# Last stage of a gated two-layer network: normed rows turned by VectorE in squares of 32, norm by ScalarE, one core

## The chip, the cores and the metric

The kernel runs on one core of a Trainium2 chip. Five instruction streams work beside each other: TensorE (PE in the profile; PEld is its weight load, which overlaps the matmuls), VectorE (DVE), ScalarE (ACT), GpSimd (POOL) and SyncE (SP), which starts transfers. Each takes its instructions in the order in which they stand in its queue and waits for the others by semaphores. The metric is the device time of one execution, in microseconds; the time before is the median of three runs.

## The reference, cut to what matters

Four layers work on `x` of 16 batches x 256 rows x 256 columns, each of them on the layernorm of the rows: cross attention, a routed feed-forward layer, masked cross attention, and a gated linear attention. The last of them is the stage that the change touches:

```
x = x + tanh(g_ffn[1]) * L1_ffn(layernorm(x))

L1_ffn(x):                     # x: [16, 256, 256], 8 heads of 64, 4 experts, chunks of 64
  q1, k1, v = x @ Wq, x @ Wk, x @ Wv
  q2 = x @ Wqa @ Wqb;  k2 = softmax(x @ Wka @ Wkb)
  gk1, gk2 = log_sigmoid(x @ Wg1a @ Wg1b + bg1) / 16, log_sigmoid(x @ Wg2a @ Wg2b + bg2) / 16
  e = softmax(x @ We);  the highest of 4 gives mask and factor
  o = gla(q1, k1, v, gk1) + sum over experts of gla(q2 * factor, k2 * factor, v, gk2 * mask)
  o = o * rsqrt(mean(o * o) + eps) * norm_w
  g = x @ Wga @ Wgb
  return (o * silu(g)) @ Wo
```

Every product with `x` needs the normed rows turned, columns across the partitions: that is the tile `xnT` below.

## The kernel before

Rows of a batch lie as a tile of 128 partitions x 2 x 256 (`xs[b]`, fp32). The stages run one after the other over all batches; stage 0 (the first attention, with the routing of the second layer beside it) takes the first 970 us or so, stages 1 and 2 end near 1240 us, the last stage's loop fills the rest. There `stage3_fast` (line 1615) is a generator whose first steps run inside the stage before.

**The loop.** Its index `p` runs from 0 to 63 (line 2015): four places per batch `b = p // 4`, place `p % 4` for a pair of heads. In each place the body issues, in this order: `start` steps, `shares` (PE: `den`), the second half of `masked` for p - 1 (DVE), `copies`, `shares_end`, in odd places `gated` (DVE: `u`), `keys_queries(p + 1)` (PE: `kq`), `middle`, `rest`, `decays(p + 1)` (PE `gq`, `gz`; ACT `ee`), `late`, `products(p, 0)` (PE `sc`), `masked(p, 0)` (DVE `at`), `behind_mask`, `factors(p + 1)` (DVE `f`), `by_rows`, `second` and `factors_second` for p + 1 (PE, ACT `e`, POOL `k`, DVE `q`), `logs`, `products(p, 1)` (PE `sc`) and `values(p - 1)` (PE `o`). In the second and third place `values` stands ahead of `second`.

**Order.** From the last stage on, every compute instruction is kept in program order on its engine (`Pinned`, line 42; `matmul` and `transpose`, lines 1632 to 1636). So the tables of steps below set the order of each queue. The profile shows all instructions of `Pinned` under line 50, the matmuls of the last stage under line 1633 and its PE transposes under line 1636.

**The tables** (lines 1968 to 1977): a place, the step, the distance `d` to the batch it works on, and arguments. `run` (line 1979) calls a step only where batch `b + d` exists.

```
start = {0: [(turn, 1)], 2: [(turn_hot, 1)]}
rest = {0: [(bias, 2)], 1: [(route, 1)], 2: [(steepest, 1, 0), (stats, 2)], 3: [(steepest, 1, 1)]}
behind_mask = {0: [(route_logits, 1)], 3: [(norm, 2)]}
logs = {0: [(route_sums, 1), (outgates_end, 0, 0)], 1: [(gate_logs, 1, 0)], 2: [(gate_logs, 1, 1)],
        3: [(outgates_end, 0, 1)]}
```

**The steps on the way of a batch's rows.** `bias` (POOL) adds to `xs[b + 2]` in the first place; `stats` in the third takes mean and variance (DVE) and makes `rs` of them (four POOL instructions: scale, and minus mean times scale); `norm` in the fourth writes `xn` with two DVE instructions that subtract the mean and multiply; `turn` in the first place of the next batch, one batch ahead, turns `xn` with four PE transposes of 128 x 128 into a PSUM bank, `tr`, which ACT copies to `xnT`. `lows(b + 1)` in the same place reads it first, then `vals` in the fourth, and `keys_queries` from there on to the third place of the batch itself.

**Buffers.** `xn` has one buffer. `xnT` has two, one for even and one for odd batches (`of`, line 1621; `w1` is opened anew at line 1999). The PSUM banks of `bank` (line 1625) are two in the loop, taken in turn by `tr`, `den`, `low`, `rt`, `zg`, `z`, `ms`, `hT`, `both`, `proj` and `v`. `sc`, the scores of `products`, has one buffer of two banks, so a `products` waits until the `masked` before it has read.

**The same work elsewhere.** `Route.turn` (line 407) with a portion turns rows in stage 0 by DVE: a square of 32 partitions x 32 columns at a place of the grid, for both halves of rows and both halves of columns in one instruction of 32 x 128, sixteen of them for a batch. `normed` (line 219) makes a norm by ACT: two instructions with scale and bias from `rs`.

Of the kernel before, what the change touches and what calls it, by code (L numbers as in the profile page):

```python
# [10 lines left out]
F32 = mybir.dt.float32  # L11
# [6 lines left out]
P = 128  # L18
B, S, D = 16, 256, 256
# [7 lines left out]
def bc(ap, shape, *axes):  # L27

    for a in axes:
        ap = ap.unsqueeze(a)  # L30
    return ap.to_broadcast(list(shape))
# [42 lines left out]
def layers(ctx: ExitStack, tc: tile.TileContext, t, out, check):  # L74
# [11 lines left out]
    xs, cs = [None] * B, [None] * B  # L86
# [17 lines left out]
    w0 = s0.enter_context(tc.tile_pool(name="s0w", bufs=1))  # L104
# [70 lines left out]
    dve, act, pool, pe = (Pinned(tc, x) for x in (nc.vector, nc.scalar, nc.gpsimd, nc.tensor))  # L175
# [43 lines left out]
    def normed(dst, src, mv, rs, p=P, n=2):  # L219
        for i in range(n):  # L220
            act.activation(dst[:, i, :], src[:, i, :], AF.Identity, bias=rs[:p, 1, i:i + 1],
                           scale=rs[:p, 0, i:i + 1])

    def softmax_last(pool, tag, src, shape):

        a = shape[1]
        mx = st.tile([P, a], F32, tag=tag + "mx", name=tag + "mx")
        dve3.tensor_reduce(mx, src, AX.X, ALU.max)
        e = pool.tile(shape, F32, tag=tag, name=tag)
        dve3.tensor_tensor(e, src, bc(mx, shape, 2), ALU.subtract)  # L230
        act3.activation(e, e, AF.Exp)
        den = st.tile([P, a], F32, tag=tag + "den", name=tag + "den")
        dve3.tensor_reduce(den, e, AX.X, ALU.add)
        dve3.reciprocal(den, den)
        pool3.tensor_tensor(e, e, bc(den, shape, 2), ALU.mult)
        return e
# [151 lines left out]
    class Route:  # L388
# [17 lines left out]

        def turn(self, b, bank, portion=None):
            if portion:

                if b not in self.xnT:  # L410
                    self.xnT[b] = ws1.tile([P, 2, S], F32, tag="rxnT", name="rxnT")
                xnT, xn = self.xnT[b], self.xn[b]
                for n in range(*portion):
                    q, r = n // 4 * 32, n % 4 * 32
                    dve.transpose(xnT[r:r + 32].rearrange("p k (i s) -> p i k s", i=2)[:, :, :, q:q + 32],
                                  xn[q:q + 32].rearrange("p i (k d) -> p i k d", k=2)[:, :, :, r:r + 32])
                return
            xnT, xn = ws1.tile([P, 2, S], F32, tag="rxnT", name="rxnT"), self.xn[b]
            self.xnT[b] = xnT
            ps = bank("rtr")  # L420
            for k in range(2):
                for i in range(2):
                    pe.transpose(ps[:, (2 * k + i) * P:(2 * k + i + 1) * P], xn[:, i, k * P:(k + 1) * P], ident)
            act.copy(xnT, ps.rearrange("p (k s) -> p k s", k=2))
# [120 lines left out]
    if fast:  # L545
        route = Route()
# [1068 lines left out]
    def stage3_fast(early_bank):  # L1615

        with ExitStack() as sx:
            w0 = w1 = sx.enter_context(tc.tile_pool(name="f3w0", bufs=1, side="right", reuse_waits="tile"))
            pss = None

            def of(b):

                return w1 if b % 2 else w0

            def bank(name):
                return pss.tile([P, 512], F32, tag="ps", name=name) if pss else early_bank(name)
# [8 lines left out]
            def transpose(*a):  # L1635
                tc.keep_in_program_order(nc.tensor.transpose(*a))
# [11 lines left out]
            xn, xnT, low, lg, hT, em, am = {}, {}, {}, {}, {}, {}, {}  # L1648
# [3 lines left out]
            mvs = {}  # L1652
# [7 lines left out]
            def norm(b):  # L1660
                x = xn[b] = w0.tile([P, 2, D], F32, tag="xn", name="xn")
                mv, rs = mvs.pop(b)
                for i in range(2):
                    dve.tensor_scalar(x[:, i, :], xs[b][:, i, :], mv[:, i, 0:1], rs[:, 0, i:i + 1],
                                      ALU.subtract, ALU.mult)

            def turn(b):
                xnT[b] = of(b).tile([P, 2, S], F32, tag="xnT", name="xnT")
                ps = bank("tr")
                for k in range(2):  # L1670
                    for i in range(2):
                        transpose(ps[:, (2 * k + i) * P:(2 * k + i + 1) * P], xn[b][:, i, k * P:(k + 1) * P], ident)
                act3.copy(xnT[b], ps.rearrange("p (k s) -> p k s", k=2))

            def lows(b):

                low[b] = of(b).tile([P, 2, S], F32, tag="low", name="low")
                ps = bank("low")
                for c in range(2):
                    for k in range(2):  # L1680
                        matmul(ps[:, c * S:(c + 1) * S], la[:, k, c * P:(c + 1) * P], xnT[b][:, k, :],
                                         start=k == 0, stop=k == 1)
                dve3.tensor_copy(low[b][:, 0, :], ps[:, :S])
                dve3.tensor_scalar(low[b][:, 1, :], ps[:, S:], vec[:, V_ONE:V_ONE + 1], None, ALU.add)
                if b > 0:
                    for r in range(0, 64, 32):
                        dve3.tensor_scalar(low2[r:r + 32, :], ps[64 + r:96 + r, S + P:],
                                           vec[64 + r:96 + r, V_ONE:V_ONE + 1], None, ALU.add)
# [149 lines left out]
            def shares(p):  # L1838

                ps = bank("den")  # L1840
                for i in range(2):
                    matmul(ps[:, 2 * i:2 * i + 2], e2[p][:, tokens(i)], halves[:, 0::64],
                                     start=True, stop=True)
                z_[p, "den"] = ps
# [34 lines left out]
            def masked(p, n):  # L1879
                b, m, cols = place(p)  # L1880
                ps = z_.pop((p, n, "sc"))
                a = w2.tile([P, 2, 384], F32, tag=f"at{n}", name=f"at{n}")
                if n == 0:
                    at[p] = a
                    dve3.tensor_tensor(a, ps[:, :, :384], bc(amask, [P, 2, 384], 1), ALU.mult)
                else:
                    r = rd.pop(p)
                    for lo, hi, i in ((0, S, 0), (S, 3 * P, 1)):
                        for j in range(2):
                            dve3.scalar_tensor_tensor(a[:, j, lo:hi], ps[:, j, lo:hi], r[:, 2 * i + j:2 * i + j + 1],  # L1890
                                                           am[b][:, lo:hi], ALU.mult, ALU.mult)
                    if p == last - 1:
                        at[p] = a
                        return
                    pool3.tensor_tensor(at[p], at[p], a, ALU.add)
# [65 lines left out]
            def warm():  # L1961

                ps = bank("warm")
                for _ in range(2):
                    matmul(ps, ones, v[B - 1][:, 0, :], start=True, stop=True)


            start = {0: [(turn, 1)], 2: [(turn_hot, 1)]}
            copies = {2: [(turned_hot, 1)]}
            middle = {0: [(lows, 1)], 1: [(all_gates, 1)], 2: [(pairs, 1)], 3: [(scaled, 0, 0)]}  # L1970

            rest = {0: [(bias, 2)], 1: [(route, 1)], 2: [(steepest, 1, 0), (stats, 2)], 3: [(steepest, 1, 1)]}
            late = {1: [(scaled, -1, 1)], 2: [(project, -1)], 3: [(vals, 1)]}
            behind_mask = {0: [(route_logits, 1)], 3: [(norm, 2)]}
            by_rows = {0: [(outgates, 0, 0)], 1: [(gates_end, 1)], 3: [(outgates, 0, 1)]}
            logs = {0: [(route_sums, 1), (outgates_end, 0, 0)], 1: [(gate_logs, 1, 0)], 2: [(gate_logs, 1, 1)],
                    3: [(outgates_end, 0, 1)]}

            def run(steps, p):
                for f, d, *a in steps.get(p % 4, ()):  # L1980
                    if 0 <= p // 4 + d < B:
                        f(p // 4 + d, *a)
# [30 lines left out]
                    squares((p - 1) // 4, (p - 1) % 4 // 2)  # L2013

            for p in range(last):
                run(start, p)
                shares(p)
                if 0 < p:
                    masked(p - 1, 1)
                run(copies, p)  # L2020
                shares_end(p)
                if 1 < p and p % 2 == 1:
                    gated((p - 2) // 4, (p - 2) % 4 // 2)
                if p + 1 < last:
                    keys_queries(p + 1)
                run(middle, p)
                run(rest, p)
                if p + 1 < last:
                    decays(p + 1)
                run(late, p)  # L2030
                products(p, 0)
                masked(p, 0)
                run(behind_mask, p)
                if p + 1 < last:
                    factors(p + 1)
                run(by_rows, p)

                inside = p % 4 in (1, 2) and p + 1 < last
                if inside:
                    summed(p)  # L2040
                if p + 1 < last:
                    second(p + 1)
                    factors_second(p + 1)
                run(logs, p)
                products(p, 1)
                if 0 < p and not inside:
                    summed(p)

            b, p = B - 1, last - 1
# [126 lines left out]
```

## Time and profile before

| | |
|---|---|
| median of three runs | 1887.42 us (1886.46 to 1890.54) |
| the profiled execution, whole time | 1884.3 us |
| its span | 1882.4 us |
| granted TensorE clock, mean of the span | 0.998 |
| PE transposes `tr` of the last stage | 64, median 273 ns |
| DVE norm `xn` of the last stage | 32, median 406 ns |
| ACT copy of `tr` to `xnT` (two stages) | 32, median 585 ns |
| busy per 40 us of the loop (1520 to 1560) | PE 40.00, DVE 26.11, ACT 18.84, POOL 18.51 us |

A timeline line reads: start (us from the span's start), duration, engine, line, operation, what is written from what, shape, how many merged into the line, and in brackets the idle time of the engine before it with what ended it. A merged line's duration is that of the whole group. A line on a tile gives minimum, median and maximum of one instruction in ns and the first and last start.

### The profile page before, as it was taken

How to read it: one execution, taken by the hardware profiler on the slowest of the kernel's cores; microseconds unless marked ns; L12 is line 12 of the kernel's file. 1: busy time of each engine (PE TensorE's matmuls, PEld its weight loads, DVE VectorE, ACT ScalarE, POOL GpSimd, SP SyncE). 2: the span in 40 equal slices, each digit the busy share in tenths (PEclk: the TensorE clock that was granted, in tenths of full speed). 3: DMA queues.
4: the chain of work that ended last, by engine and by line, in shares of the span. 5: the costliest groups of instructions: out<-in, count | busy, mean ns of one | idle time of the engine just before them, and what ended most of it. 6: DMA issues, size and time to landing. Idle time of an engine off the chain costs nothing.

```text
span 1882.4 us, 35167 instructions
## 1 busy us (share of the span) xinstructions
PE 1857.9 (99%) x13862; PEld 1301.3 (69%) x13862; DVE 1142.9 (61%) x2787; ACT 858.6 (46%) x1790; POOL 1024.0 (54%) x1049
## 2 busy tenths in 40 slices
PE   8999999999999999999999999999999999999997
PEld 5666676666666666666787766567777777777775
DVE  3345656556556666654573588876666666666654
ACT  4333344443434343443333587745444444454453
POOL 4654757566676567665725666124444444444433
PEclk9999999999999999999999999999999999999999
DMA  9500000100010000000179733000000000000000
GB/s 320 199 3 19 29 21 15 34 10 22 23 34 11 27 16 12 27 30 12 37 256 258 175 48 50 3 1 7 7 7 7 12 7 6 7 7 7 12 6 14
DMA packets 56903, 84.64 MB, mean 45 GB/s; under 512 B 10467, under 2 KB 44371, under 8 KB 56217
## 3 DMA queue, kind: packets, MB, share of 16 engines
q1 hardware_dynamic: 44441, 65.52, 10.4%
q0 software_dynamic: 12288, 16.79, 4.4%
q8 instruction: 111, 1.82, 0.4%
q14 instruction: 63, 0.52, 0.1%
HBM read 44.00 MB, written 38.29 MB: 44 GB/s over the span
## 4 chain that ended last, share of the span: by engine, by line
PE 93%; DVE 2%; ACT 1%; POOL 1%; issue 1%; DMA 0%; SPq 0%; POOLq 0%; ACTq 0%; DVEq 0%
PE o L50 13%; PE qk L50 13%; PE sc L50 10%; PE v L50 8%; PE proj L50 7%; PE kq L1633 6%; PE sc L1633 5%; PE gq L1633 3%; PE ex L50 3%; PE v L1633 3%; PE proj L1633 3%; PE o L1633 3%; PE gz L1633 2%; PE den L1633 2%; PE low L1633 1%; PE ms L1633 1%
## 5 line engine op out<-in xcount | busy, mean ns | idle before, releaser
L50 POOL TENSOR_SCALAR rs<-mv 128x2 f32<-128x2 f32 (+2 forms) x85 | 16.2, 191 | 401.0 <-DVE mv L50 394.9
L50 DVE RECIPROCAL rd<-o 128x256 f32<-128x256 f32 x64 | 112.4, 1756 | 172.4 <-PE o L50 137.5
L50 ACT ACTIVATE e<-sc 128x1024 f32<-128x1024 f32 (+1 forms) x192 | 181.6, 1015 | 18.5 <-PE sc L50 18.5
L50 PE MATMUL sc<-qk 64*128 64x256 f32 (+1 forms) x1536 | 183.1, 384 | 0.5 <-DVE qk L50 0.5
L50 PE MATMUL o<-e,v 128*32 128x256 f32 (+1 forms) x3072 | 177.9, 379 | 0.0
L50 PEld LDWEIGHTS sc<-qk 64*128 64x128 f32 (+1 forms) x1536 | 132.0, 172 | 55.1 <-issue 26.8
L50 POOL TENSOR_TENSOR esum<-esum,es 128x512 f32<-128x512 f32 x128 | 163.0, 1274 | 10.0
L50 PE MATMUL qk<-kvT,wkv 128*128 128x333 f32 x512 | 164.3, 443 | 0.0
L50 POOL TENSOR_TENSOR es<-e 128x1024 f32<-128x1024 f32 x64 | 151.2, 2363 | 13.8 <-ACT e L50 10.7
L50 POOL TENSOR_TENSOR es<-es,e 77x1024 f32<-77x1024 f32 x64 | 150.3, 2349 | 5.0
L50 ACT ACTIVATE qk<-qk 128x256 f32<-128x256 f32 x128 | 48.9, 382 | 227.1 <-PE qk L50 227.1
L50 PEld LDWEIGHTS o<-e,v 128*32 128x32 f32 (+1 forms) x3072 | 99.8, 110 | 66.4
L50 POOL TENSOR_TENSOR k<-e,ee 128x256 f32<-128x256 f32 x64 | 46.7, 730 | 181.3 <-ACT e L50 181.3
L50 PE MATMUL qk<-kvT,wq 128*128 128x256 f32 x512 | 134.3, 385 | 0.0
L50 DVE TENSOR_TENSOR at<-sc,amask 128x768 f32<-128x768 f32 x64 | 61.3, 957 | 113.4 <-PE sc L1633 109.7
L50 DVE COPY qk<-qk 128x333 f32<-128x333 f32 x128 | 64.6, 505 | 106.0 <-ACT qk L50 104.5
L50 POOL TENSOR_TENSOR at<-at,at 128x768 f32<-128x768 f32 x63 | 113.8, 1807 | 23.5 <-DVE at L50 23.5
L50 POOL DMA_INDIRECT x<-rows_out,pos x64 | 101.0, 1579 | 36.8 <-issue 16.5
L50 PEld LDWEIGHTS qk<-kvT,wkv 128*128 128x128 f32 x512 | 97.2, 190 | 30.0
L50 PEld LDWEIGHTS qk<-kvT,wq 128*128 128x128 f32 x512 | 94.4, 189 | 33.8 <-issue 13.7
L50 PE MATMUL proj<-wo0h,oT 128*128 128x256 f32 x512 | 113.5, 380 | 0.0
L50 PE MATMUL v<-wkv,kvT 128*128 128x512 f32 x256 | 113.0, 594 | 0.0
(256 smaller groups left out, 4148.7 us busy)
## 6 DMA issues: line engine op xcount, KB each, us to landing
rows<-zero SPq DMA_DIRECT2D x16, 640.0 KB
xin<-rows SPq DMA_DIRECT2D x16, 640.0 KB
rows_out<-y SPq DMA_DIRECT2D x16, 384.0 KB
v<-vctx SPq DMA_DIRECT2D x15, 308.0 KB
x<-in_x_dram SPq DMA_DIRECT2D x16, 256.0 KB
rows_out<-y SPq DMA_DIRECT2D x16, 256.0 KB
out_dram<-x SPq DMA_DIRECT2D x15, 256.0 KB
wkv<-in_wkv_dram SPq DMA_DIRECT2D x2, 1024.0 KB
```

The source lines that it names most:

```text
L50: x = getattr(self.engine, name)(*a, **k)
L1633: tc.keep_in_program_order(nc.tensor.matmul(*a, **k))
```

## The change

The steps `norm` and `turn` of batches 2 to 15 are replaced. `norm_ahead` stands in the third place behind the second `gate_logs`, and writes `xn` by ACT with `normed`. `turn_ahead` stands in the fourth place behind the second `steepest`, ahead of `decays`, and writes `xnT` of two batches ahead with sixteen DVE instructions. `turn` by PE is left for batch 0, ahead of the loop, and for batch 1, at p = 0; `norm` by DVE is left for batches 0 and 1. The body of `Route.turn` is moved into the function `turned_squares`, with nothing else changed for stage 0.

```
+    def turned_squares(xT, x, portion):
+        for n in portion:
+            q, r = n // 4 * 32, n % 4 * 32
+            dve.transpose(xT[r:r + 32].rearrange("p k (i s) -> p i k s", i=2)[:, :, :, q:q + 32],
+                          x[q:q + 32].rearrange("p i (k d) -> p i k d", k=2)[:, :, :, r:r + 32])
...
-                for n in range(*portion):
...
+                turned_squares(self.xnT[b], self.xn[b], range(*portion))
...
+            def norm_ahead(b):
+                xn[b] = w0.tile([P, 2, D], F32, tag="xn", name="xn")
+                normed(xn[b], xs[b], *mvs.pop(b))
...
+            def turn_ahead(b):
+                xnT[b] = of(b).tile([P, 2, S], F32, tag="xnT", name="xnT")
+                turned_squares(xnT[b], xn[b], range(16))
...
-            start = {0: [(turn, 1)], 2: [(turn_hot, 1)]}
+            start = {2: [(turn_hot, 1)]}
...
-            rest = {..., 3: [(steepest, 1, 1)]}
+            rest = {..., 3: [(steepest, 1, 1), (turn_ahead, 2)]}
...
-            behind_mask = {0: [(route_logits, 1)], 3: [(norm, 2)]}
+            behind_mask = {0: [(route_logits, 1)]}
...
-            logs = {..., 2: [(gate_logs, 1, 1)], ...}
+            logs = {..., 2: [(gate_logs, 1, 1), (norm_ahead, 2)], ...}
...
             for p in range(last):
+                if p == 0:
+                    turn(1)
                 run(start, p)
```

More of the change, by code (lines that the diff above doesn't have):

```diff
@@ L411, in turn @@
                     self.xnT[b] = ws1.tile([P, 2, S], F32, tag="rxnT", name="rxnT")
-                xnT, xn = self.xnT[b], self.xn[b]
-                for n in range(*portion):
-                    q, r = n // 4 * 32, n % 4 * 32
-                    dve.transpose(xnT[r:r + 32].rearrange("p k (i s) -> p i k s", i=2)[:, :, :, q:q + 32],
-                                  xn[q:q + 32].rearrange("p i (k d) -> p i k d", k=2)[:, :, :, r:r + 32])
+                turned_squares(self.xnT[b], self.xn[b], range(*portion))
                 return
@@ L1965, in warm @@
                     matmul(ps, ones, v[B - 1][:, 0, :], start=True, stop=True)
-            start = {0: [(turn, 1)], 2: [(turn_hot, 1)]}
+            start = {2: [(turn_hot, 1)]}
             copies = {2: [(turned_hot, 1)]}
             middle = {0: [(lows, 1)], 1: [(all_gates, 1)], 2: [(pairs, 1)], 3: [(scaled, 0, 0)]}
-            rest = {0: [(bias, 2)], 1: [(route, 1)], 2: [(steepest, 1, 0), (stats, 2)], 3: [(steepest, 1, 1)]}
+            rest = {0: [(bias, 2)], 1: [(route, 1)], 2: [(steepest, 1, 0), (stats, 2)], 3: [(steepest, 1, 1), (turn_ahead, 2)]}
             late = {1: [(scaled, -1, 1)], 2: [(project, -1)], 3: [(vals, 1)]}
-            behind_mask = {0: [(route_logits, 1)], 3: [(norm, 2)]}
+            behind_mask = {0: [(route_logits, 1)]}
             by_rows = {0: [(outgates, 0, 0)], 1: [(gates_end, 1)], 3: [(outgates, 0, 1)]}
-            logs = {0: [(route_sums, 1), (outgates_end, 0, 0)], 1: [(gate_logs, 1, 0)], 2: [(gate_logs, 1, 1)],
+            logs = {0: [(route_sums, 1), (outgates_end, 0, 0)], 1: [(gate_logs, 1, 0)], 2: [(gate_logs, 1, 1), (norm_ahead, 2)],
                     3: [(outgates_end, 0, 1)]}
```

## The prediction

> **What bounds the kernel now.** I read the page's first part, the busy time by window, the timeline of one batch, then the waits of the last stage.
>
> ```profile
> PE 1857.9 (99%) x13862; PEld 1301.3 (69%) x13862; DVE 1142.9 (61%) x2787; ACT 858.6 (46%) x1790; POOL 1024.0 (54%) x1049
> ```
> ```profile
> 1480.00:1520.00 40.00, 40.00 (x258) 30.01 (x257) 26.12 (x67) 18.84 (x43) 18.52 (x22) 1.00 0.02 8
> ```
>
> The columns of the second line are the window, then busy time of PE, PEld, DVE, ACT and POOL, the granted clock, DMA share and GB/s. One batch of the last stage takes 39.77 us (matmuls of `kq` of the same place start at 1327.60 and 1367.37 in the chain of waits), and PE is busy in all of it at clock 1.00. So an instruction taken from PE is worth its own time, as long as no other engine makes PE wait; DVE has about 14 us idle per batch, but its queue is in order, so what counts is where they lie. This is the third place's end, the fourth place and the start of the next first place, around the batch's `turn`, and then the second place for comparison:
>
> ```profile
> 1505.00 1.05 ACT L50 ACTIVATE lg<-lg 128x1024 f32<-128x1024 f32 x1
> ...
> 1507.39 1.21 DVE L50 TENSOR_REDUCE gates<-lg 128x1 f32<-128x1024 f32 x1
> ...
> 1508.57 0.69 ACT L50 ACTIVATE r<-ms,eps 128x512 f32<-128x512 f32 x1 [2.52 <-PE ms L1633]
> ...
> 1510.09 1.27 POOL L50 TENSOR_TENSOR oT<-u,r 128x512 f32<-128x512 f32 x1 [1.29 <-ACT r L50]
> ...
> 1512.79 0.92 PE L1633 MATMUL sc<-f 64*128 64x256 f32 x8
> ...
> 1513.83 0.96 DVE L50 TENSOR_TENSOR at<-sc,amask 128x768 f32<-128x768 f32 x1 [5.23 <-PE sc L1633]
> ...
> 1514.70 0.73 DVE L50 TENSOR_SCALAR xn<-x,mv,rs 128x256 f32<-128x256 f32 x2
> 1514.90 0.76 PEld L1633 LDWEIGHTS sc<-q,k 64*128 64x128 f32 x8 [0.30 <-issue]
> ...
> 1515.79 0.87 PE L1633 MATMUL o<-at,v 128*64 128x256 f32 x8
> ...
> 1516.59 0.66 PE L1636 MATMUL tr<-ident,xn 128*128 128x128 f32 x4
> ...
> 1517.28 0.58 ACT L50 COPY xnT<-tr 128x512 f32<-128x512 f32 x1 [0.62 <-PE tr L1636]
> ...
> 1517.55 1.11 PE L1633 MATMUL kq<-xnT,wk 128*128 128x256 f32 x4
> ...
> 1525.06 0.87 PE L1633 MATMUL o<-at,v 128*64 128x256 f32 x8
> ...
> 1526.33 1.11 PE L1633 MATMUL kq<-xnT,wk 128*128 128x256 f32 x4
> ```
>
> Two things to see: DVE stands still for 5.23 us in the fourth place, from the end of `gates` (1508.60) until the scores `sc` come (1513.83), while PE does the eight `v` matmuls; and ACT stands still for 2.52 us just before, from the end of `lg` (1506.05) to 1508.57. The waits by engine name the same idle stretch in every batch (`at` behind `sc`, longest 5.2 us).
>
> The operations that come in run in the first stage already, through the same code on the same shapes:
>
> ```profile
> L50 DVE STREAM_TRANSPOSE rxnT<-rxn x224: 287/303/308, 111.9 to 876.2; 32x128 f32<-32x128 f32 x112
> ...
> L50 ACT ACTIVATE xn<-x,rs x32: 587/596/601, 1035.0 to 1199.0; 128x256 f32<-128x256 f32 x32
> ```
> ```profile
> 402.57 0.69 DVE L50 TENSOR_TENSOR oT<-o,rd 128x512 f32<-128x512 f32 x1
> 403.17 2.50 DVE L50 STREAM_TRANSPOSE rxnT<-rxn 32x128 f32<-32x128 f32 x8
> 405.69 0.69 DVE L50 COPY v<-v 128x512 f32<-128x512 f32 x1
> ```
>
> **How often.** Batch 0 is turned ahead of the loop, batch 1 still by PE at p = 0. The steps moved are those of batches 2 to 15: 14 times.
>
> **Removed: four PE transposes.** From the start of `o` to the start of the next `kq` the first place takes 1517.55 - 1515.79 = 1.76 us with the transposes, the second place, same instructions without them, 1526.33 - 1525.06 = 1.27 us. So 0.49 us each. Bounds: 0.44 us, four steps of 0.11 us such as the chain of waits gives one `gz` matmul just before, and 0.58 us, what the same chain gives `tr`. 14 x 0.49 = **6.9 us** (6.2 to 8.1).
>
> **Removed: ACT's copy of the bank (0.58 us) and DVE's norm (two of 0.41, 0.65 us until the next starts).** Neither engine bounds PE there, so I count nothing. DVE's `f`, `q` and the masks after them come 0.65 us sooner, and the cover they had stays.
>
> **Added: 16 squares on DVE.** Eight take 2.50 us, so one follows another after (2.50 - 0.303)/7 = 0.314 us and sixteen take 15 x 0.314 + 0.303 = 5.01 us. They stand behind `gates`: from 1508.60 at the latest to 1513.61. The instruction behind them is `at` (`masked`, first half), which waited for `sc` until 1513.83 anyway: 0.22 us to spare, or 0.30 if the first square begins before `gates` has ended, as the first behind `oT` does (403.17 against 403.26). Behind `at`, PE waits with the second `sc` for the one buffer that `at` reads: `at` ends at 1513.83 + 0.96 = 1514.79, PEld goes on at 1514.90, and elsewhere in the batch 0.05 us lies between the two, so another 0.06 us. From a delay of about 0.3 us on, every microsecond of DVE is one of PE, 14 times. I count nothing. With each square at the longest seen (308 ns) the sixteen take 5.09 us, still inside; without any cover they would cost 14 x 5.01 = 70 us.
>
> The Trainium skill (VectorE: DVE Perf Modes, "Rules for kernel authors") speaks against the move: it says to turn 128x128 on TensorE where PSUM will do. On their own engines the rows agree, 0.49 us against 5.01 us; on that reckoning, with nothing hiding the squares, 14 x (5.01 - 0.49) = 63 us would be lost.
>
> **Added: norm on ACT.** Two of 596 ns, 1.19 us, behind the `lg` that ends at 1506.05: done by 1507.3, inside the 2.52 us that ACT idles, and 1.2 us ahead of the squares, which can't start before 1508.52. It needs `rs`, whose last step POOL starts at 1502.18 (0.22 us). Cost nothing; behind it ACT has `r`, which waits for PE until 1508.57. If the cover went, `r` and `oT` would be late, and `oT` has until the next `project`, over 20 us on.
>
> **Moved: buffers and banks.** The squares of b+2 write the buffer of xnT[b], whose last readers are the `kq` matmuls of the third place, over 10 us earlier. The two rotating PSUM banks lose one user per batch: `den` now follows the second `v` (copied by 1513.48), `low` follows `zg` (copied by DVE at 1516.96, sooner by 0.65), and PE reaches `low` near 1518.9. No new wait. No DMA is issued by a moved step, and neither SP's nor POOL's queue is passed.
>
> **Sum.** Span 1882.4 - 6.9 = 1875.5, for that execution 1884.3 - 6.9 = 1877.4 us. The profiled execution lies 3.1 us below the median of the three timed runs (1887.42); against that, **1880.5 us** (1879.3 to 1881.2 by the bounds of the PE term).
>
> **Rivals.**
> - *The squares overrun a little.* The fit is 5.01 us in 5.23, so a start 0.4 us late or squares of 0.34 us make PE wait. 0.5 us per batch past the slack gives all of it back: 14 x 0.5 = 7.0, 1887.5 us; 0.25 us per batch leaves 1884. For it: the slack of 0.3 us; against it: 224 squares between 287 and 308 ns.
> - *Another wait takes the PE time.* `den` in the first place comes 0.49 us sooner and reads `e`, which ACT ends at 1515.48; that is 1.1 us ahead of the new start. 1886 to 1888 if something of the kind holds PE.
> - *Slower: POOL blocks DVE.* POOL multiplies `oT` (1.27 us) in the middle of the squares, from 1510.09. If a square can't run beside it, the sixteen end at 1513.61 + 1.27 = 1514.88, 1.05 us after 1513.83; less the 0.06 us that PE has, PE waits about 1.0 us: 14 x (1.0 - 0.49) = 7.1, **1894.5 us**. It decides from 0.49 us of stall on. Against it: in the first stage POOL ran `es` from 402.99 to 405.33 across all of the eight squares shown, and they kept to 0.314 us. For it: nothing but that POOL's operations there are others.
> - *Slower: no cover at all.* If the squares came on PE's path whole, 1887.4 + 63 = 1950. Nothing in the timeline says so.
>
> The Trainium skill (SBUF — State Buffer, "Who interferes with whom") has the rule behind the third: a VectorE instruction in a two-port mode and a GpSimd one shut each other out for a whole instruction, while one with a single SBUF input outside these modes does not contend. It doesn't list the transpose among those that enter the mode, and the trace of the first stage agrees that it does not.
>
> **How the numbers follow.** Forecast 0.64; small overrun 0.14; another wait 0.06; POOL's block 0.14; no cover 0.02. A measurement of this kernel tells about 0.2%, 3.8 us, from no change. Faster by more: the forecast and the mildest of the overruns, 0.67. Within 0.2%: 0.17. Slower: 0.16. The range reaches from the PE term's larger bound and 1.3 us of spread below, 1878, to 1889, which takes in the overrun and the other wait and leaves out the slower pair and a small tail below.
>
> **What would show it.** PE with 56 instructions fewer; 224 squares `xnT<-xn` at 303 ns in the fourth place; the idle time before `at` there down from 5.23 to about 0.2 us, with `sc` still its releaser; no wait of PE or PEld for DVE `at`; the distance from batch to batch 39.3 us. I am wrong if PE's second `sc` in the fourth place starts later behind the first `sc` than now (1514.93 - 1512.79 = 2.14 us), if the squares show gaps beside `oT`, or if the squares begin behind ACT's norm instead of behind `gates`.

## The result, and the profile after

| | before | after |
|---|---|---|
| median, first measurement (7 runs each) | 1886.46 us | 1878.49 us |
| ratio | | 0.9960, 95% interval 0.9951 to 0.9969 |
| median, measured again (15 and 5 runs) | 1884.75 us | 1878.19 us |
| ratio | | 0.9964, interval 0.9950 to 0.9977 |
| span of the profiled execution | 1882.4 us | 1878.0 us; 1874.9 us in the second measurement |

The kernel became 8.0 us faster in the first measurement and 6.6 us in the second; the forecast was 6.9.

The page's first part, the kernel after (busy time, share of the span, instructions):

```profile
PE 1853.7 (99%) x13806; PEld 1297.6 (69%) x13806; DVE 1204.0 (64%) x2983; ACT 864.3 (46%) x1804; POOL 1025.0 (55%) x1049
```

PE has 56 matmuls fewer, DVE 196 instructions and 61 us more, on a kernel that got faster. Where the 61 us went shows the timeline of the kernel after, from the third place's end to the second `kq` of the next batch:

```profile
1505.46 1.08 ACT L50 ACTIVATE xn<-x,rs 128x256 f32<-128x256 f32 x2
...
1506.90 1.21 DVE L50 TENSOR_REDUCE gates<-lg 128x1 f32<-128x1024 f32 x1
...
1508.03 5.03 DVE L50 STREAM_TRANSPOSE xnT<-xn 32x128 f32<-32x128 f32 x16
1508.08 0.69 ACT L50 ACTIVATE r<-ms,eps 128x512 f32<-128x512 f32 x1 [1.54 <-PE ms L1635]
...
1509.59 1.27 POOL L50 TENSOR_TENSOR oT<-u,r 128x512 f32<-128x512 f32 x1 [1.28 <-ACT r L50]
...
1512.29 0.92 PE L1635 MATMUL sc<-f 64*128 64x256 f32 x8
...
1513.34 0.96 DVE L50 TENSOR_TENSOR at<-sc,amask 128x768 f32<-128x768 f32 x1 [0.28 <-PE sc L1635]
...
1514.44 0.92 PE L1635 MATMUL sc<-q,k 64*128 64x256 f32 x8
...
1515.29 0.87 PE L1635 MATMUL o<-at,v 128*64 128x256 f32 x8
...
1516.56 1.11 PE L1635 MATMUL kq<-xnT,wk 128*128 128x256 f32 x4
```

The squares fill the gap that was 5.23 us and leave 0.28 us of it; `sc` still ends DVE's wait. The second `sc` follows the first after 2.15 us, as before (2.14). From `o` to `kq` it is now 1.27 us instead of 1.76. The chain of waits of the kernel after gives the batch's length from the `kq` of two first places (start, duration, what):

```profile
1359.55 1.83 PE kq L1635 x8
...
1398.84 1.83 PE kq L1635 x8
```

39.29 us against 39.77, so 0.48 us less, 14 times: 6.7 us. No run says where the 1.3 us more of the first measurement come from. The profile shown here gained only 4.4 us of span, because of a stretch ahead of the long run of equal batches. The windows (window; its length; busy time of PE, PEld, DVE, ACT, POOL; granted clock; DMA share; GB/s) of this execution and of the second measurement's:

```profile
1240.00:1245.00 5.00, 4.71 (x16) 3.79 (x16) 3.90 (x7) 1.02 (x3) 1.75 (x3) 0.56 0.01 2
```
```profile
1240.00:1245.00 5.00, 4.07 (x23) 3.36 (x22) 3.37 (x7) 0.97 (x2) 2.15 (x3) 1.00 0.01 2
```

The same code ran at a granted clock of 0.56 in one execution and of 1.00 in the other. PE reaches the loop's first `gq` at 1248.64 us in the first case and at 1245.83 in the second; in the profile before, at a clock of 1.00, it does so at 1246.21. These 2.8 us are most of the 3.1 us between the two spans of the changed kernel.

### The profile page after: what moved, and what is told of

Read it like the earlier page. It is cut to its first block, busy times and chain, and to the rows that moved or that the text cites. A ratio compares the mean times of both kernels' runs of the same rounds, so it can differ in the third digit from the quotient of the medians.

```text
span 1878.0 us, 35237 instructions
## 1 busy us (share of the span) xinstructions
PE 1853.7 (99%) x13806; PEld 1297.6 (69%) x13806; DVE 1204.0 (64%) x2983; ACT 864.3 (46%) x1804; POOL 1025.0 (55%) x1049
## 4 chain that ended last, share of the span: by engine, by line
PE 93%; DVE 2%; ACT 2%; POOL 1%; issue 1%; DMA 0%; SPq 0%; POOLq 0%; ACTq 0%
PE o L50 13%; PE qk L50 13%; PE sc L50 10%; PE v L50 9%; PE proj L50 7%; PE kq L1635 6%; PE sc L1635 5%; PE gq L1635 3%; PE v L1635 3%; PE ex L50 3%; PE proj L1635 3%; PE o L1635 3%; PE gz L1635 2%; PE den L1635 2%; PE low L1635 2%; PE ms L1635 1%
## 5 line engine op out<-in xcount | busy, mean ns | idle before, releaser
L50 PEld LDWEIGHTS proj<-wo0h,oT 128*128 128x128 f32 x512 | 95.9, 190 | 13.4 <-issue 0.8
```

The lines of the kernel that those rows point to most:

```text
L50: x = getattr(self.engine, name)(*a, **k)
```

## The experiments

Each kernel was timed beside the kernel before, on the same chip. "Changed" is the kernel after. All ratios are to before. Where a kernel is set against the changed one, the changed one's first median (1878.49 us) is meant unless the text says otherwise; the kernel before had medians from 1884.75 to 1886.46 us on these occasions, so I trust such a difference to some 2 us, and the batch's length in the trace more.

**Norm alone.**

```
start = {0: [(turn, 1)], 2: [(turn_hot, 1)]}
rest = {..., 3: [(steepest, 1, 1)]}
logs = {..., 2: [(gate_logs, 1, 1), (norm_ahead, 2)], ...}
```

> Norm alone moved to ScalarE in the third place; the rows are turned by PE in the first place as before. Theory (the gain is the PE time of the four transposes, 0.48 us x 14): no change against before, within 1.5 us; the fourth place shows DVE idle 5.23 us before `at` as before. Rival (the gain comes from DVE being rid of the norm, whose 0.65 us stood between `at` and `f`): 3 to 7 us faster than before.

Measured 1884.71 us against 1885.49; ratio 0.9993 (0.9985 to 1.0002), which doesn't tell it from no change. DVE's wait in the fourth place is 5.2 us as before. The trace tells more than the time: the batch takes 39.68 us, 0.09 less than before, with PE's transposes, the copy by ScalarE and the order of the banks left as they were (chain of waits):

```profile
1519.35 1.83 PE kq L1635 x8
...
1559.03 1.83 PE kq L1635 x8
```

So freeing DVE of the norm is worth 0.09 us per batch, 14 x 0.09 = 1.3 us. They lie in the first place, where `o` to `kq` takes 1.66 us here and 1.76 before. In the kernel before, the bank that `den` takes is the one of `zg`, which DVE copies to `zs` behind the norm. The weights of `den` are loaded when that copy has just ended, 0.49 us behind those of `tr` (timeline of the kernel before, then of this one):

```profile
1516.28 0.68 DVE L50 COPY zs<-zg 128x512 f32<-128x512 f32 x1
1516.59 0.42 PEld L1636 LDWEIGHTS tr<-ident,xn 128*128 128x128 f32 x4 [0.17 <-issue]
...
1517.08 0.52 PEld L1633 LDWEIGHTS den<-halves,e 128*128 128x128 f32 x4
```
```profile
1518.35 0.42 PEld L1638 LDWEIGHTS tr<-ident,xn 128*128 128x128 f32 x4 [0.17 <-issue]
...
1518.74 0.53 PEld L1635 LDWEIGHTS den<-halves,e 128*128 128x128 f32 x4
```

With the norm gone from DVE the copy ends at 1518.08, well ahead of the load, and the load follows that of `tr` after 0.39 us. A short wait of `den` for its bank fits this; no run tests it by itself.

**PE's transposes put back, unread.** `turn` without the copy stands in the first place, and the squares stay.

> The changed kernel, and PE makes its four transposes of each batch as well, in the first place as before, into a bank that nothing copies. Theory: 0.48 us x 14 = 6.7 us slower than the changed kernel, so 0 to 1 us faster than before. Rival (part of the gain is the copy by ScalarE, the rotation of the banks or DVE's shorter queue): clearly faster than before, by 3 us or more.

Measured 1884.62 us against 1886.40; ratio 0.9990 (0.9981 to 0.9999): 6.1 us slower than the changed kernel. The batch takes 39.68 us (first places at 1519.84 and 1559.52), so the transposes alone cost 0.39 of the 0.48 us. The other 0.09 us are the norm's: with the norm alone moved the batch took 39.68 us too. Between these two kernels the copy went and the squares came, and the batch's length stayed the same.

**One square more, four squares more.**

```
turned_squares(xnT[b], xn[b], [*range(16), *range(1)])     # the other: *range(4)
```

> The changed kernel with one square of each batch done twice (17 instead of 16). Theory: 0.314 us more against 0.28 us of idle time and 0.06 us behind it: no wait of PE, as fast as the changed kernel within 1 us (6.5 to 8 us faster than before); idle before `at` gone in the fourth place. Rival (DVE's time counts as such): 14 x 0.314 = 4.4 us slower than the changed kernel.

> The changed kernel with four squares of each batch done twice (20 instead of 16). Theory: 1.26 us more, less 0.34 us, so 0.92 us of waiting for PE in each of 14 batches: 12.9 us slower than the changed kernel, 5 to 6 us slower than before; PEld waits for DVE `at` ahead of the second `sc` of the fourth place, 0.9 us each time. Rival (PE makes part of it good later in the batch, where DVE stands idle again): less than 6 us slower than the changed kernel, still faster than before.

One more: 1879.85 us against 1885.49, ratio 0.9966 (0.9953 to 0.9979), with the batch at 39.29 us as in the changed kernel, seventeen squares in 5.38 us and no wait of PE for `at`. Four more: 1895.77 us, ratio 1.0054 (1.0041 to 1.0067), 10.3 us slower than before. The waits of PE in the loop of that kernel are one line (who waited for whom, us in total, times, longest):

```profile
PE sc L1635 <- DVE at L50: 14.3, 13, 1.1
```

1.1 us each instead of the 0.92 forecast: the twenty squares took 6.44 us, 1.41 more than the sixteen instead of 1.26. `at` started 1.15 us later behind the first `sc` than in the changed kernel (2.20 instead of 1.05), the second `sc` 1.16 us (3.31 instead of 2.15). So 1.41 - 1.16 = 0.25 us of the delay were covered. The kernel with one more gives another figure: its squares took 0.35 us more and cost nothing, as its `at` began 0.06 us before the last square had ended. The slack lies between 0.25 and 0.35 us; whether the 0.06 us behind `at` are part of it stays open. PE made nothing good later in the batch.

**The squares behind `at`.**

```
rest = {..., 3: [(steepest, 1, 1)]}
behind_mask = {0: [(route_logits, 1)], 3: [(turn_ahead, 2)]}
```

> The same sixteen squares as in the changed kernel, same place of four, but behind `at` (the first half of `masked`) instead of ahead of it. Same work on each engine. Theory: DVE's 5.2 us of idle time are ahead of `at` and are not used now; `f`, which clears the bank that the next `kq` writes, starts 5.03 us later (1519.2 instead of 1514.2 in the timeline), ends 1519.9, while PE reaches `kq` at 1516.6: PE waits 3.4 us in each of 14 batches, 45 to 50 us slower than the changed kernel, about 40 slower than before. Rival (the load of DVE counts, not the place): as the changed kernel.

Measured 1951.23 us against 1886.40, ratio 1.0342 (1.0326 to 1.0358): 73 us slower than the changed kernel with the same instructions on the same engines. The wait is as worked out (waits, then timeline):

```profile
PEld kq L1635 <- DVE f L50: 40.9, 12, 3.4
```
```profile
1506.63 1.87 PE L1635 MATMUL kq<-xnT,wk 128*128 128x256 f32 x4 [3.33 <-DVE f L50]
1508.30 1.91 PE L1635 MATMUL kq<-xnT,wq 128*128 128x256 f32 x4
```

The columns of the first are the total, the times and the longest, in the loop from 1270 to 1800 us. But 73/14 = 5.2 us per batch is more than 3.4. The windows of the same kernel within that wait and behind it show the rest:

```profile
1504.00:1506.00 2.00, 0.00 (x0) 0.00 (x0) 1.90 (x7) 0.00 (x0) 0.00 (x0) 1.00 0.00 0
...
1508.00:1509.00 1.00, 1.00 (x4) 0.81 (x3) 0.97 (x5) 0.00 (x0) 1.00 (x2) 0.50 0.00 0
```

After 3.33 us without work PE runs at half its clock; the eight `kq` matmuls take 3.58 us in the chain of waits instead of 1.83. With 3.4 that makes 5.2. Read in windows of half a microsecond, the clock is at 0.50 for 3.4 us behind each of the twelve waits in the loop. The Trainium skill (TensorE: Matmul & The Clock Gate, "Why this matters for your kernels") says to leave no gaps of over some 3 us between bursts of matmuls, as the clock falls to half behind one; this trace agrees with 3.33 us.

**The same with PE kept busy.** Six matmuls of 512 columns ahead of `den` in the first place, into a bank that nothing reads.

> The kernel with the squares behind `at`, with six matmuls of 512 columns more in the first place ahead of `den`, 2.6 us in all, into a bank that nothing reads: PE's idle time before `kq` falls from 3.33 us to about 0.7 us, and the work that `kq` waits for is as late as it was. Theory (3.4 us of the 5.2 us per batch is the wait, the rest is the clock, 0.50 for some 4 us behind each wait): the clock stays at 1.00, 14 x 3.4 = 48 us slower than the changed kernel, about 1926 us, 25 us faster than without the matmuls. Rival (DVE's lateness costs all of the 5.2 us): about 1951 us, or more by the added matmuls.

Measured 1951.57 us against 1884.75, ratio 1.0352 (1.0336 to 1.0368). I had mis-sized the filling: each of the six stands as two in the trace, and the twelve take 5.35 us, not 2.6, which is more than the whole gap (chain of waits):

```profile
1501.38 5.35 PE tr L1635 x12
```

The granted clock is 1.00 in the loop, PE waits for DVE no more, and the eight `kq` take 1.83 us again, but the filling itself costs 14 x 5.35 = 75 us. The time is the one that the rival named, by way of the added matmuls. The run shows that the slow stretch goes when PE doesn't stand still; it doesn't show what a filling that fits would give, and so doesn't decide between the two.

**Norm by DVE at the end of the third place.**

```
logs = {..., 2: [(gate_logs, 1, 1), (norm, 2)], ...}
```

> Squares as in the changed kernel, norm by DVE, in the place where the changed kernel has ScalarE's. Theory: DVE's queue is 0.65 us later at the squares; the idle time before `at` was 0.28 us and PE has 0.06 us behind it, so PE waits 0.65 - 0.34 = 0.31 us in each of 14 batches: 4.3 us slower than the changed kernel, 2.5 to 4 us faster than before. Rival (the fit in DVE's gap is not tight, or does not decide): as fast as the changed kernel, 7 to 8 us faster than before.

Measured 1888.12 us against 1885.49, ratio 1.0014 (1.0005 to 1.0023): slower than before, 9.6 us slower than the changed kernel and not 4.3. The second `sc` follows the first after 2.86 us, 0.71 more than in the changed kernel, x 14 = 9.9 us. The norm itself had become longer (timeline, then the line of the tile with minimum, median and maximum in ns):

```profile
1508.50 1.25 DVE L50 TENSOR_SCALAR xn<-x,mv,rs 128x256 f32<-128x256 f32 x2
1508.55 0.73 POOL L50 TENSOR_TENSOR k<-e,ee 128x256 f32<-128x256 f32 x1 [2.80 <-ACT e L50]
```
```profile
L50 DVE TENSOR_SCALAR xn<-x,mv,rs x26: 400/664/931, 1308.5 to 1789.4; 128x256 f32<-128x256 f32 x26
```

Two instructions of 406 ns took 1.25 us: the first of them 0.93 us, from 1508.50, while POOL did `k`. Hence the next run.

**Norm by DVE where POOL stands idle.**

```
behind_mask = {0: [(route_logits, 1)], 2: [(norm, 2)]}
logs = {..., 2: [(gate_logs, 1, 1)], ...}
```

> Squares as in the changed kernel, norm by DVE, but in the third place behind the first half of `masked` instead of at the place's end. In the run with it at the end one of the two `xn` instructions took up to 931 ns instead of 406, while POOL did `k` (0.73 us); here POOL stands idle beside it. Theory (DVE waits for POOL there): both take 0.41 us, DVE's queue is 0.65 us later at the squares instead of 1.17, PE waits 0.65 - 0.28 = 0.37 us instead of 0.71 us: 5.2 us slower than the changed kernel, 2 to 3 us faster than before. Rival (the norm is longer for another reason and what is late stays late): 1 to 3 us slower than before, as with the norm at the end.

Measured 1880.57 us against 1884.75, ratio 0.9979 (0.9970 to 0.9988): 4.2 us faster than before, 2.4 slower than the changed kernel timed beside it (1878.19 us). The tile's line in this kernel:

```profile
L50 DVE TENSOR_SCALAR xn<-x,mv,rs x26: 402/405/409, 1305.0 to 1779.0; 128x256 f32<-128x256 f32 x26
```

Same instructions, same engine, 7.5 us apart (batches of 40.00 and 39.47 us); beside the one pair a POOL instruction ran, beside the other none. The Trainium skill (SBUF — State Buffer, "Who interferes with whom") names `tensor_scalar` among the VectorE operations that can take the port pair shared with GpSimd, and says that whoever issues first keeps the pair while the other is blocked for the whole instruction. The two lines agree that the two hinder each other. The order they don't bear out: DVE's record begins 0.05 us ahead of POOL's `k` and is the one that became longer. The squares don't behave so: in the kernel after they kept 5.03 us across POOL's `oT`. The delay was smaller than I expected (0.19 us more between the two `sc` instead of 0.37): DVE had 0.14 us of idle time ahead of the second half of `masked` that took up some of it.

**The choice of expert turned by DVE too.** `hot` lies in a cleared tile of 32 columns, and `turn_hot` moves to the second place behind `route`:

```
x = of(b).tile([32, 2, P], F32, tag="hT", name="hT")
for q in range(0, P, 32):
    dve.transpose(x[:, :, q:q + 32], hots[b % 2][q:q + 32])
```

> The changed kernel, and the choice of expert (`hot`, 4 columns in a cleared tile of 32) turned by DVE too: four squares of 32x64 in the second place behind `route`, in place of two PE transposes and DVE's copy in the third. Theory: PE gets 0.13 us in the third place (start of `sc` to start of `kq` 1.31 us there, 1.18 us in the fourth, which has no transposes), x 15 = 2.0 us; DVE has 1.44 us of idle time in the second place and needs about 0.9 us: 9 to 10 us faster than before. Rival (the squares don't fit or PE's gap stays): 6 to 8 us faster than before.

> The changed kernel again, for comparison on the same chip with the run after it: 7 to 8 us faster than before.

> The changed kernel with the choice of expert turned by DVE as well, again: 1.7 to 2.1 us faster than the changed kernel (the batch takes 39.18 us instead of 39.29, and what it took off the median). Rival (the first measurement was chance): the same as the changed kernel within 1 us.

First 1876.40 us against 1886.40, ratio 0.9944 (0.9931 to 0.9958). Again, beside each other: the changed kernel 1878.19 us (6.6 us faster than before, not 7 to 8), this one 1874.94 us, before 1884.75; ratios 0.9964 (0.9950 to 0.9977) and 0.9948 (0.9934 to 0.9962). The intervals overlap. The medians differ by 2.1 us across the two occasions and by 3.3 us beside each other, more than the 1.7 to 2.1 expected. What the trace bears out is the batch, 39.18 us instead of 39.29 (first places at 1514.98 and 1554.16), x 15 = 1.7 us. DVE in the second place:

```profile
1489.01 0.97 DVE L50 STREAM_TRANSPOSE hT<-hot 32x64 f32<-32x64 f32 x4
1490.42 0.96 DVE L50 TENSOR_TENSOR at<-sc,amask 128x768 f32<-128x768 f32 x1 [0.44 <-PE sc L1635]
```

0.44 us of the 1.44 are left: it fits. This kernel has the lowest median of all that were timed.

**The logits of the routing as well.** Four more squares in the first place, behind `at`.

```
rows = low[b][64:96, 1, :].rearrange("p (i s) -> p i s", i=2)
for q in range(0, P, 32):
    dve.transpose(x[q:q + 32], rows[:, :, q:q + 32])
```

> The kernel before this one, and the logits of the routing turned by DVE as well: four squares of 32x64 behind `at` in the first place, in place of two PE transposes of 64x128. Theory: PE gains 0.12 us in the first place (what the chain of waits gives `rt`), but DVE is about 0.85 us later in the first place and has 1.44 us less 0.9 us left in the second: over by about 0.3 us, so PE waits 0.2 to 0.3 us there: 0 to 3 us slower than the kernel before this one. Rival (small squares are shorter than 0.2 us each, all fits): 1.8 us faster than it.

Measured 1887.26 us against 1886.40, ratio 1.0007 (0.9998 to 1.0016): 10.9 us slower than the kernel before this one, neither what the theory nor what the rival gave. The squares take 0.98 us, and what waits for them is not what I had thought of (timeline of this kernel):

```profile
1531.31 0.21 ACT L50 ACTIVATE e<-e 128x8 f32<-128x8 f32 x1 [2.57 <-DVE e L50]
...
1531.90 0.38 ACT L50 ACTIVATE e<-gz 128x256 f32<-128x256 f32 x1
...
1532.33 0.61 PE L1635 MATMUL den<-halves,e 128*128 128x2 f32 x4 [0.59 <-ACT e L50]
```

The exponential of the routing waits on ACT for DVE, and behind it in ACT's order stands the `e` that PE's next `den` reads. PE waits 0.59 us there, 13 times in the loop.

## Why the prediction was right

The forecast was 1880.5 us, a fall of 6.9 us; measured were 1878.49 us and falls of 8.0 and 6.6 us. The forecast started from the median of three runs, 1887.42 us; the seven of the first measurement have 1886.46, so about half of the 2 us by which the forecast lies too high is its starting point. Step by step:

- **PE sets the time, and four transposes cost it 0.49 us.** The batch got 0.48 us shorter, so the sum holds, but it wasn't all the transposes'. They take 0.39 us, below the lower bound of 0.44. The other 0.09 us came with the norm, which the prediction counted at nothing. The total was right because the stretch it was read from, `o` to `kq`, holds both: it takes 1.76 us before, 1.66 with the norm moved alone, 1.27 with the transposes gone as well.
- **Sixteen squares take 5.01 us from the end of `gates`.** 5.03 us; the first began 0.08 us before `gates` had ended, the case for which I gave 0.30 us of slack. 0.28 us were left.
- **From 0.3 us of delay on, a microsecond of DVE is one of PE.** One square more (0.35 us) cost nothing in the batch's length, four more (1.41 us) made it 1.16 us longer at the second `sc`, 17 us in all.
- **No cover would cost 70 us.** Behind `at` the squares cost 73 us, but that the figures lie so close is chance: they are made of 3.4 us of wait and 1.75 us of halved clock, 14 times. I had no term for the clock.
- **ACT's norm costs nothing.** It took 1.08 us of the 2.52 us idle and left 1.54. The price of not doing it there, which I had not worked out, is 2.4 us at the better place on DVE and 9.6 us at the worse.
- **POOL's block of DVE** did not happen to the squares: sixteen in 5.03 us across `oT`. The row that I held against it was read a little too widely (`es` ended at 405.33 us, before the eighth square began), which changes nothing. What the rival feared did happen to `tensor_scalar` where it ran beside `k`.
- **Another wait** did not come: PE and PEld show no longer wait than before in the first place. One small wait seems to have gone, the one of `den`.

The range went up to 1889 for overruns that stayed away; the measured time lay 0.5 us above its lower end.

## What to carry to other kernels

Where one engine is busy throughout, its work can go to an engine that takes over ten times as long for it (5.03 us against 0.39 us) if that engine has one idle stretch in its own order that is long enough. What counts is the length of that stretch against the work, ahead of which instruction it lies, and who waits behind: the same squares one instruction later cost 73 us. Behind every delayed instruction look for the waits two engines on, as in the routing's exponential, which held PE by standing in front of another in ACT's queue. And a difference between two stretches of a trace is the price of everything that differs between them: here a run with one of the two parts moved was needed to split 0.48 us into 0.39 and 0.09.

## What the runs showed of the hardware

With the squares behind `at`, each wait of PE of some 3.3 us was followed by 3.4 us at a granted clock of 0.50, not by the 4 us that I had expected, in all twelve batches between 1270 and 1800 us. Half of 3.4 us is 1.7 us, so each of these waits cost half as much again. A DVE `tensor_scalar` of 405 ns took up to 931 ns beside POOL's `k`, while the `STREAM_TRANSPOSE` kept its 302 ns (287 to 308) across POOL's `oT`. The squares of 32x64 took 232 ns, those of 32x128 302 ns, so twice the columns cost 30% more.
